# Four images of self-attention on one core: the last group's shared bank added before the next image's first projection

## Chip, core and metric

The kernel runs on one core of one Trainium2 chip. The metric is the device time of one execution in microseconds (us); the time before is the median of three executions. The engines are named as in the profile: PE is TensorE's matmul stream, PEld its weight loads, DVE is VectorE, ACT is ScalarE, POOL is GpSimd and SP is SyncE. GpSimd and SyncE mostly issue transfers here. [...]

## What is computed

Four images of 64 x 64 positions with 256 channels, in float32. Each is projected to queries and keys of 128 channels and values of 256, attends to itself with a softmax over 4096 positions, and is added to its input:

```python
q = jnp.einsum('bwhc,cd->bwhd', x, Wq) + bq
k = jnp.einsum('bwhc,cd->bwhd', x, Wk) + bk
v = jnp.einsum('bwhc,cd->bwhd', x, Wv) + bv
pq = q.reshape(B, -1, N)      # B = 4, N = 4096; a reshape, not a transpose
pk = k.reshape(B, -1, N)
pv = v.reshape(B, -1, N)
energy = jnp.einsum('bcn,bcm->bnm', pq, pk)
attention = jax.nn.softmax(energy, axis=-1)
out = jnp.einsum('bcm,bnm->bcn', pv, attention)
return gamma * out.reshape(B, W, H, C) + x
```

## The kernel before

The kernel splits each float32 operand into parts that TensorE can multiply as fp32r, so that a product becomes three matmuls. For each image it first projects 16 blocks `i` of the image (transposes on TensorE, then `qk`, then `v`), and then runs 16 groups `g` of 256 queries. A group takes 8 steps; a step computes energies and exponentials three steps ahead and attends with what is ready. The attention of a group collects in three PSUM banks: two sums `acc[0]`, `acc[1]` of the upper parts, and one bank `bb` that both halves of the queries share, for the difference part. At a group's last step ScalarE copies the two sums to `o`:

```python
# end of attend(b, u), at a group's last step
o = now["o"] = work.tile([P, NJ, C + 2], F32, tag="o", name=f"o_{b}_{g}")
for j in range(NJ):
    nc.scalar.activation(o[:, j, :], acc[j], AF.Identity, scale=1.0 + E)      # L385
```

The rest of a group's end is a generator, whose pieces are emitted one at a time between other work. `start` runs it to its first `yield`; each `proceed` emits the next piece:

```python
def start(pieces):
    active.append(pieces)
    next(pieces)

def proceed():
    for pieces in list(active):
        if next(pieces, StopIteration) is StopIteration:
            active.remove(pieces)

def finish(b, g, o, bb, xr):
    yield
    yield
    nc.vector.tensor_copy(zall[:, b * NG + g, :], o[:, :, C])                 # L398
    r, _ = factors(b, g, gam1)                       # L390 reciprocal, L391 multiply (DVE)
    nc.vector.tensor_tensor(o[:, :, :C], o[:, :, :C], bb, ALU.add)            # L400
    yield
    for j in range(NJ):
        nc.scalar.activation(                                                 # L403
            o[:, j, :C], o[:, j, :C], AF.Identity, scale=r[:, j : j + 1])
    yield
    yield
    tp = ps_t.tile([P, 2, NB], F32, tag="t", name=f"ot_{b}_{g}")
    for s in range(2):
        for j in range(NJ):
            nc.tensor.transpose(                                              # L411
                tp[:, s, j * P : (j + 1) * P], o[:, j, s * P : (s + 1) * P], ident)
    yield
    nc.vector.tensor_tensor(xr, xr, tp, ALU.add)                              # L415
    nc.gpsimd.dma_start(ov[b, g], xr)                                         # L416
```

The projection of one block, and the splitting of its keys, are these; `halved` makes the parts of a tile, the first on ScalarE and two on DVE:

```python
def transposed(self, i):                   # of Projection, cut
    for g in range(i, i + 2):
        self.load(g)                       # x of this block and the next, on SyncE (L82)
    ...                                    # four transposes on TensorE           (L124)
    nc.scalar.copy(self.xt[i], tp)         #                                       L130

def qk(self, i):                           # of Projection, cut
    ...                                    # matmuls                              (L137)
    nc.vector.tensor_tensor(dst, qk[...], bqk_sb[...], ALU.add)                 #  L146

def halved(f, x):
    h = f[:, :, 0, :]
    nc.scalar.activation(h, x, AF.Identity, scale=UPPER / 64)                   #  L263
    for j, s, op in ((1, -64.0, ALU.add), (2, 64.0 * (1.0 + E), ALU.subtract)):
        nc.vector.scalar_tensor_tensor(                                         #  L265
            f[:, :, j, :], h.bitcast(F32), s, x, ALU.mult, op)

def project_qk(b, i):
    images[b].qk(i)
    x = now["qk"]
    for s in range(2):
        nc.gpsimd.dma_start(qd[b, i // 2 + NG // 2 * s][:, i % 2, :], x[:, s, :C2])   # L273
    f = kpool.tile([P, 2, 3, P], F32R, tag="f", name=f"f_{b}_{i}", bufs=2)
    halved(f, x[:, :, C2:])
    nc.gpsimd.dma_start(kf[b, i // 2][:, i % 2], f.rearrange("p s j d -> p s (j d)")) # L276
```

The loop over the images puts these together. The first two blocks of an image are transposed, and the first is projected to q and k, at the end of the image before:

```python
for b in range(B):
    pr = images[b]
    ...                                    # b == 0: the same for the first image
    for i in range(1, NI):                 # the projections, NI = 16
        ...
        if i + 1 < NI:
            pr.transposed(i + 1)
        while i == 1 and active:
            proceed()                      # emits all that is left of the last group
        begin(b, i)
        project_qk(b, i)
        ...
        project_v(b, i - 1)                # matmuls L158, ScalarE L167
        proceed()
    project_v(b, NI - 1)
    for u in range(STEPS):                 # the attention, STEPS = 128
        ...
        attend(b, u)                       # matmuls L374
        if (b, u) == (B - 1, STEPS - 1):
            finish_last(b, g, loads.pop((b, "x", g)))
        elif t == NU - 1:
            start(finish(b, g, now["o"], now["bb"], loads.pop((b, "x", g))))
        proceed()
    if b + 1 < B:
        images[b + 1].transposed(1)
        project_qk(b + 1, 0)
```

For the PSUM tiles of these first blocks the kernel takes turns between the two double-buffered banks of the energies; from `i == 3` it uses the banks of the attention.

Of the kernel before, what the change touches and what calls it, by code (L numbers as in the profile page):

```python
# [20 lines left out]
def kernel(  # L21
# [58 lines left out]
    def load_x(pool, b, g):  # L80
        t = pool.tile([P, 2, XB], F32, tag="x", name=f"x_{b}_{g}")
        nc.sync.dma_start(t, xv[b, g])  # L82
        return t
# [117 lines left out]
    with ExitStack() as fast:  # L201
# [30 lines left out]
# [9 lines that stand above are left out]
        def image(b):  # L241
            def xt_out(i):
                return xtpool.tile([P, KC, 2, P], F32, tag="xt", name=f"xts_{b}_{i}")

            def qk_out(i):
                now["qk"] = work.tile([P, 2, 2 * C2], F32, tag="qk", name=f"qks_{b}_{i}")
                return ((now["qk"], 0),)

            def v_out(i):
                now["v4"] = work.tile([P, KC, C], F32, tag="v4", name=f"v4_{b}_{i}")  # L250
                return now["v4"], bv4_sb, 1.0 / E

            images.append(Projection(b, xpool, lambda: next(now["banks"]), xt_out, qk_out, v_out))

            for g in range(NG):
                qd[b, g] = dram.tile([P, NJ, P], F32, tag=f"qd{g}", name=f"qd_{b}_{g}")
            for t in range(NU):
                kf[b, t] = dram.tile([P, 2, 2, 3 * P], F32R, tag=f"kf{t}", name=f"kf_{b}_{t}")

        def halved(f, x):  # L260

            h = f[:, :, 0, :]
            nc.scalar.activation(h, x, AF.Identity, scale=UPPER / 64)  # L263
            for j, s, op in ((1, -64.0, ALU.add), (2, 64.0 * (1.0 + E), ALU.subtract)):
                nc.vector.scalar_tensor_tensor(  # L265
                    f[:, :, j, :], h.bitcast(F32), s, x, ALU.mult, op
# [11 lines that stand above are left out]
        def project_v(b, i):  # L278
            images[b].v(i)
            units[b, "v4", i] = now["v4"]  # L280
            if i < NI - 2:
                halve_v(b, i)
# [12 lines left out]
        def load_q(b, g):  # L295
            t = work.tile([P, NJ, P], F32, tag="qr", name=f"qr_{b}_{g}", bufs=1)
            nc.sync.dma_start(t, qd[b, g])
            loads[b, "qr", g] = t
# [12 lines left out]
        def energy(b, u, k):  # L311

            g, t = divmod(u, NU)
            if k == 0:
                x = ppool.tile([P, 4, NB], F32, tag="x", name=f"x_{b}_{u}", bufs=3)
                y = ppool.tile([P, 4, NB], F32, tag="y", name=f"y_{b}_{u}")
                units[b, u] = x, y
            x, y = units[b, u]
            q, kt = loads[b, "q", g], loads[b, "k", u]
            sa = ps_s.tile([P, 2, NJ, P], F32, tag="a", name=f"sa_{b}_{u}_{k}")  # L320
            sb = ps_s.tile([P, 2, NJ, P], F32, tag="b", name=f"sb_{b}_{u}_{k}")
            for i in range(2):
                for to, f, first, last in ((sa, 0, True, False), (sa, 1, False, True), (sb, 2, True, True)):
                    nc.tensor.matmul(  # L324
                        to[:, i], kt[:, 2 * k + i, f, :], q[:, f], start=first, stop=last
                    )
            for to, sp, scale in ((x, sa, (1.0 + E) / E), (y, sb, -1.0 / E)):
                nc.scalar.activation(  # L328
                    to[:, 2 * k : 2 * k + 2, :],
                    sp.rearrange("p i j d -> p i (j d)"),  # L330
                    AF.Exp,
                    scale=scale,
                )

        def join(b, u):

            x, y = units[b, u]
            nc.vector.tensor_tensor(x, x, y, ALU.mult)  # L338
            units[b, u] = x

        def upper(b, u):
            h = ppool.tile([P, 4, NB], F32R, tag="h", name=f"h_{b}_{u}", bufs=3)
            nc.scalar.activation(h, units[b, u], AF.Identity, scale=UPPER)  # L343
            units[b, u] = units[b, u], h

        def halves(b, u):
            x, h = units[b, u]
            l = ppool.tile([P, 4, NB], F32R, tag="l", name=f"l_{b}_{u}")
            nc.vector.tensor_tensor(l, x, h.bitcast(F32), ALU.subtract)  # L349

            d = ppool.tile([P, 4, NB], F32R, tag="d", name=f"d_{b}_{u}")
            nc.vector.scalar_tensor_tensor(  # L352
                d, h.bitcast(F32), 1.0 + E, x, ALU.mult, ALU.subtract
            )
            units[b, u] = h, l, d
# [106 lines left out]
        def begin(b, i):  # L462

            if i == 5:
                load_q(b, 0)
            if i == 9:
                halve_q(b, 0)
            if i in (4, 6, 8):
                load_k(b, i // 2 - 2)
            if i >= 10:  # L470
                energy(b, (i - 10) // 2, i % 2)
            if i in (12, 14):
                join(b, i // 2 - 6)
            if i in (13, 15):
                upper(b, i // 2 - 6)
                load_k(b, i // 2 - 3)

        image(0)
        for b in range(B):
            pr = images[b]  # L480
            if b == 0:
                now["banks"] = energies
                pr.transposed(0)
                pr.transposed(1)
                project_qk(b, 0)
            for i in range(1, NI):
                if i == 3:
                    now["banks"] = outputs
# [6 lines that stand above are left out]
                if i == NI - 1:  # L495
                    halves(b, 0)
                project_v(b, i - 1)
                proceed()
            project_v(b, NI - 1)
            for u in range(STEPS):  # L500
                g, t = divmod(u, NU)
                ahead = u + LOOK
                if ahead // NU + 1 < NG and ahead % NU == 3:
                    load_q(b, ahead // NU + 1)
                if u == STEPS - NU and b + 1 < B:
                    image(b + 1)
                if u >= STEPS - 3 and b + 1 < B:
                    now["banks"] = energies
                    if u == STEPS - 3:
                        images[b + 1].load(0)  # L510
                    elif u == STEPS - 2:
                        images[b + 1].transposed(0)
                if t == NU - 3:
                    loads[b, "x", g] = load_x(xpool, b, g)
                for k in range(2):
                    if ahead < STEPS:
                        energy(b, ahead, k)
                    if k == 0 and u + 2 < STEPS:
                        join(b, u + 2)
                        upper(b, u + 2)  # L520
                load_k(b, ahead + 2)
                proceed()
                if u + 1 < STEPS:
                    halves(b, u + 1)
                if ahead // NU + 1 < NG and ahead % NU == 5:
                    halve_q(b, ahead // NU + 1)

                if u in (1, 3):
                    halve_v(b, NI - 2 + u // 2)
                attend(b, u)  # L530
# [3 lines that stand above are left out]
                    start(finish(b, g, now["o"], now["bb"], loads.pop((b, "x", g))))  # L534
                proceed()
            if b + 1 < B:
                images[b + 1].transposed(1)
                project_qk(b + 1, 0)

    NB = 512  # L540
    NG = N // NB
# [132 lines left out]
```

## Time and profile before

| what | value |
|---|---|
| time, median of 3 | 2474.3 us (2473.92 to 2475.12) |
| profiled execution, first to last instruction | 2471.3 us |
| mean granted TensorE clock | 0.996 |
| TensorE matmul busy | 2447.6 us, 99% |
| VectorE busy | 2095.9 us, 85% |
| ScalarE busy | 1805.7 us, 73% |
| GpSimd busy | 425.7 us, 17% |
| bytes moved by DMA | 498.92 MB, mean 202 GB/s |

Busy time is what an engine's instructions cover; idle time of an engine that does not set the pace costs nothing. The wait list gives, for an instruction and what released it, the total, the number and the longest of the idle times. The granted clock is the share of TensorE's full clock that the chip allowed in a stretch. A line of the timeline gives the start, the duration, the engine, the line in the kernel, the operation, its output and inputs by name with their shapes, how many instructions are merged, and in brackets the idle time before it with its releaser. The line numbers L385 to L416 stand beside the code above.

### The profile page before, as it was taken

The numbers are of one execution on the slowest core, as the hardware profiler recorded it, in microseconds if no ns is written. First come the engines' busy times: TensorE is split into PE (matmuls) and PEld (weight loads), VectorE is DVE, ScalarE is ACT, GpSimd is POOL, SyncE is SP. The second block draws the span as 40 slices with busy tenths as digits, with TensorE's granted clock in tenths as the row PEclk, the third lists the DMA queues.
The fourth block names the chain that finished last, engine by engine and source line by source line (L and its number), as shares of the span: only waits on it lengthen the run. The fifth ranks groups of instructions, "written<-read, shape, count | busy, mean of one in ns | idle before, by whom it ended". The sixth has DMA issues, their size and how long they took to land.

```text
span 2471.3 us, 50024 instructions
## 1 busy us (share of the span) xinstructions
PE 2447.6 (99%) x19982; PEld 2412.5 (98%) x19982; DVE 2095.9 (85%) x2314; ACT 1805.7 (73%) x3201; POOL 425.7 (17%) x781
## 2 busy tenths in 40 slices
PE   9999999999999999999999999999999999999998
PEld 8999999999899999999989999999998999999998
DVE  5888888888698888888769888888876988888887
ACT  5777777776677777777657777777766777777775
POOL 4211111111411111111131111111114111111110
PEclk9999999999999999999999999999999999999999
DMA  7666666664766666666477666666647766666663
GB/s 234 220 204 204 208 206 205 198 211 144 237 215 198 206 210 204 207 202 207 142 226 216 204 201 209 204 211 201 207 141 224 224 205 198 208 206 205 209 201 111
DMA packets 137408, 498.92 MB, mean 202 GB/s; under 512 B 15536, under 2 KB 57264, under 8 KB 137168
## 3 DMA queue, kind: packets, MB, share of 16 engines
q0 software_dynamic: 92320, 453.17, 58.8%
q1 hardware_dynamic: 44304, 42.22, 5.6%
q8 instruction: 160, 2.62, 0.4%
q14 instruction: 80, 0.66, 0.1%
q10 hardware_dynamic: 544, 0.26, 0.0%
HBM read 445.25 MB, written 50.33 MB: 201 GB/s over the span
## 4 chain that ended last, share of the span: by engine, by line


## 5 line engine op out<-in xcount | busy, mean ns | idle before, releaser
L328 ACT ACTIVATE x<-sa 128x512 f32<-128x512 f32 x1024 | 612.9, 599 | 494.9 <-PE sa L324 491.7
L338 DVE TENSOR_TENSOR x<-x,y 128x1024 f32<-128x1024 f32 x512 | 626.4, 1223 | 188.0 <-ACT y L328 188.0
L324 PE MATMUL sa<-q,k 128*128 128x256 f32 x4096 | 736.6, 279 | 1.1 <-ACT x L328 1.1
L352 DVE SCALAR_TENSOR_TENSOR d<-h,x 128x1024 fp32r<-128x1024 f32 x512 | 624.4, 1219 | 0.0
L349 DVE TENSOR_TENSOR l<-x,h 128x1024 fp32r<-128x1024 f32 x512 | 624.3, 1219 | 0.0
L324 PEld LDWEIGHTS sa<-q,k 128*128 128x128 f32 x4096 | 619.5, 188 | 2.4 <-ACT x L328 1.9
L328 ACT ACTIVATE y<-sb 128x512 f32<-128x512 f32 x1024 | 614.6, 600 | 0.0
L374 PE MATMUL a<-vh,h 128*128 128x258 f32 x4096 | 574.4, 283 | 0.0
L374 PE MATMUL a<-vl,l 128*128 128x258 f32 x4096 | 572.8, 282 | 0.0
L324 PE MATMUL sb<-q,k 128*128 128x256 f32 x2048 | 567.6, 277 | 0.0
L343 ACT ACTIVATE h<-x 128x1024 fp32r<-128x1024 f32 x512 | 544.6, 1064 | 23.1 <-DVE x L338 19.2
L374 PE MATMUL bb<-vd,d 128*128 128x256 f32 x4096 | 558.6, 279 | 0.0
L308 POOL DMA_DIRECT2D k<-kf x512 | 280.0, 547 | 1575.4 <-PE sb L324 1550.4
L374 PEld LDWEIGHTS a<-vl,l 128*128 128x128 f32 x4096 | 525.3, 189 | 0.0
L374 PEld LDWEIGHTS a<-vh,h 128*128 128x128 f32 x4096 | 522.9, 189 | 0.0
L374 PEld LDWEIGHTS bb<-vd,d 128*128 128x128 f32 x4096 | 515.1, 188 | 0.0
L324 PEld LDWEIGHTS sb<-q,k 128*128 128x128 f32 x2048 | 384.5, 188 | 0.9 <-ACT y L328 0.8
L137 PE MATMUL qk<-wqk_sb,xts 128*128 128x256 f32 x512 | 124.4, 387 | 0.0
L158 PE MATMUL v<-xts,wv_sb 128*128 128x256 f32 x512 | 121.2, 381 | 0.0
L158 PEld LDWEIGHTS v<-xts,wv_sb 128*128 128x128 f32 x512 | 98.2, 192 | 13.7
L137 PEld LDWEIGHTS qk<-wqk_sb,xts 128*128 128x128 f32 x512 | 94.5, 194 | 10.7
L273 POOL DMA_DIRECT2D qd<-qks x128 | 69.1, 544 | 187.3 <-DVE qks L146 178.1
(56 smaller groups left out, 869.7 us busy)
## 6 DMA issues: line engine op xcount, KB each, us to landing
k<-kf POOLq DMA_DIRECT2D x512, 768.0 KB, 4.7
x<-in_x_dram SPq DMA_DIRECT2D x128, 256.0 KB, 3.4
kf<-f POOLq DMA_DIRECT2D x64, 384.0 KB, 3.7
out_dram<-x POOLq DMA_DIRECT2D x63, 256.0 KB, 2.5
qd<-qks POOLq DMA_DIRECT2D x128, 64.0 KB, 2.8
qr<-qd SPq DMA_DIRECT2D x64, 128.0 KB, 2.6
wv_sb<-in_L_conv_Wv_dram POOLq DMA_DIRECT2D x1, 256.0 KB, 5.8
out_dram<-x SPq DMA_DIRECT2D x1, 256.0 KB, 3.7
```

What stands on the lines that cost most here:

```text
L137: nc.tensor.matmul(qk[:, s, :], self.xt[i][:, k, s, :], wqk_sb[:, k, :], start=(k == 0), stop=(k == KC - 1),)
L158: nc.tensor.matmul(vp[:, eh, :], wv_sb[:, k, eh * P : (eh + 1) * P], self.xt[i][:, k].rearrange("p s a -> p (s a)"), start=(k == 0), stop= ...
L273: nc.gpsimd.dma_start(qd[b, i // 2 + NG // 2 * s][:, i % 2, :], x[:, s, :C2])
L308: nc.gpsimd.dma_start(t.rearrange("p (i s) f d -> p i s (f d)", s=2), kf[b, u % NU])
L324: nc.tensor.matmul(to[:, i], kt[:, 2 * k + i, f, :], q[:, f], start=first, stop=last)
L328: nc.scalar.activation(to[:, 2 * k : 2 * k + 2, :], sp.rearrange("p i j d -> p i (j d)"), AF.Exp, scale=scale,)
L338: nc.vector.tensor_tensor(x, x, y, ALU.mult)
L343: nc.scalar.activation(h, units[b, u], AF.Identity, scale=UPPER)
L349: nc.vector.tensor_tensor(l, x, h.bitcast(F32), ALU.subtract)
L352: nc.vector.scalar_tensor_tensor(d, h.bitcast(F32), 1.0 + E, x, ALU.mult, ALU.subtract)
L374: nc.tensor.matmul(out_, left[:, i, j * P : (j + 1) * P], right[:, m, : out_.shape[1]], start=(t == i == 0 and (left is h or left is d and ...
```

## The change

At the end of an image (but not of the last one) two `proceed()` are put around the next image's second block of transposes and first projection. The finishing group stands behind its first two `yield`s there. The first `proceed()` emits its third piece, the copy of the softmax sums, the factors and the add of the shared bank, ahead of the projection's work on DVE. The second emits the scaling on ScalarE behind the projection's. What is left, the transposes, the add to the input and the store, is emitted where it was, in the next image's first loop turn, behind the transposes of block 2. No instruction is added or left out. The purpose is that the shared bank, which is complete before the projection begins, is used at once.

```diff
@@ -534,8 +534,10 @@
                     start(finish(b, g, now["o"], now["bb"], loads.pop((b, "x", g))))
                 proceed()
             if b + 1 < B:
+                proceed()
                 images[b + 1].transposed(1)
                 project_qk(b + 1, 0)
+                proceed()
 
     NB = 512
     NG = N // NB
```

## The prediction

> **What bounds the kernel now.** I read the page's busy times first, then TensorE's waits, then the timeline at an image's end, then the granted clock there. The changed lines run only where `b + 1 < B`, so three times: at the ends of images 0, 1 and 2. The first line of the page says that TensorE is the bound and that almost nothing is left on it:
>
> ```profile
> PE 2447.6 (99%) x19982; PEld 2412.5 (98%) x19982; DVE 2095.9 (85%) x2314; ACT 1805.7 (73%) x3201; POOL 425.7 (17%) x781
> ```
>
> PE idles for 2471.3 - 2447.6 = 23.7 us in all. Its waits (us in total, times, longest) say on what; the largest one concerns exactly this change:
>
> ```profile
> PE ot L411 <- ACT o L403: 10.0, 3, 3.3
> PE wp L199 <- POOL ident masks.py:199: 2.4, 1, 2.4
> PE sa L324 <- ACT x L328: 1.1, 4, 0.3
> ```
>
> Three waits of 3.3 us: the transposes of the finished group (L411) wait for ScalarE's scaling (L403). They come 63 times; only the three at image ends wait. The timeline of the first image end shows why (start, duration, engine, line, then the idle time before it and its releaser):
>
> ```profile
> 615.19 1.09 PE L374 MATMUL bb<-vd,d 128*128 128x256 f32 x8
> ...
> 618.28 0.60 PE L124 MATMUL xt<-ident,x 128*128 128x128 f32 x4
> 618.48 0.69 DVE L146 TENSOR_TENSOR qks<-qk,bqk_sb 128x512 f32<-128x512 f32 x1 [6.00 <-PE qk L137]
> 619.21 0.42 ACT L263 ACTIVATE f<-qks 128x256 fp32r<-128x256 f32 x1 [1.87 <-DVE qks L146]
> ...
> 619.53 0.57 ACT L130 COPY xts<-xt 128x512 f32<-128x512 f32 x1
> 619.66 0.76 DVE L265 SCALAR_TENSOR_TENSOR f<-f,qks 128x256 fp32r<-128x256 f32 x2 [0.48 <-ACT f L263]
> 620.34 0.23 DVE L398 COPY zall<-o 128x2 f32<-128x2 f32 x1
> ...
> 620.88 0.68 DVE L400 TENSOR_TENSOR o<-o,bb 128x512 f32<-128x512 f32 x1
> ...
> 621.65 0.91 ACT L403 ACTIVATE o<-o,r 128x256 f32<-128x256 f32 x2 [1.55 <-DVE o L400]
> ...
> 622.21 0.95 PE L411 MATMUL ot<-ident,o 128*128 128x128 f32 x4 [3.33 <-ACT o L403]
> ```
>
> The bank `bb` is complete at 615.19 + 1.09 = 616.28, yet DVE adds it (L400) only at 620.88: it stands in DVE's program behind the next image's first projection (L146, L265), for which DVE sat idle 6.00 us. PE has nothing after its transposes at 618.88 until 622.21.
>
> The wait has a second price that the wait table does not show. The granted clock in 2 us stretches after the stall (us, busy times by engine, then PEclk, DMA share and GB/s) at the first, second and third image end:
>
> ```profile
> 622.00:624.00 2.00, 1.71 (x9) 1.42 (x10) 0.69 (x1) 0.56 (x2) 0.00 (x0) 1.00 0.57 197
> ...
> 1237.00:1239.00 2.00, 2.00 (x6) 1.56 (x5) 0.59 (x1) 0.00 (x0) 0.68 (x1) 0.50 0.00 0
> ...
> 1854.00:1856.00 2.00, 2.00 (x7) 1.55 (x6) 0.00 (x0) 0.00 (x0) 0.68 (x1) 0.50 0.27 96
> ```
>
> After the second and third stalls PE runs at half clock. From the first L411 transpose to the next image transpose (L124, x_3) took 622.21 to 626.46 = 4.25 us at the first end, 1235.56 to 1242.68 = 7.12 us at the second and 1852.14 to 1858.07 = 5.93 us at the third: 2.87 and 1.68 us more for the same instructions, 4.55 us in this execution.
>
> [...] two idle times of 3.33 us were followed by a clock of 0.50 and one was not. [...] L400 had all its inputs at 616.3 and started at 620.88, behind L265. [...] here the same 8 matmuls count 1.89 us at full clock and 3.62 us at half (second image end), both as "busy", so I look at the clock as well as at the gaps.
>
> **The change part by part.** Nothing is added or removed: the order of TensorE's, GpSimd's and the DMA queue's instructions is the same. On DVE, at three places, L398, L390, L391 and L400 move ahead of L146 and the two L265. On ScalarE the two L403 move ahead of the copy of x_2's transposes (L130), but remain behind the first projection's L263. Worked at the first end:
>
> - DVE: the two evacuations L385 start at 614.91 and take 0.87, to 615.78. L398 follows at about 615.8; from L398 to L400 was 0.54 us (620.34 to 620.88), so L400 is ready at 616.35 and bb is too (616.28). With a hand-over of 0.05 us: 616.4 to 617.1. PE delivers the first projection for L146 at 618.48 as before, so four instructions move into idle time, cost nothing, and leave DVE 1.4 us early.
> - ScalarE: L263 still starts at 619.21, because it waits for L146. L403 now takes the place that L130 had behind it, 619.53 instead of 621.65: 2.12 us earlier. The same subtraction gives 1234.99 - 1232.87 = 2.12 at the second end and 1851.58 - 1849.46 = 2.12 at the third.
> - PE: L411 began 622.21 - 621.65 = 0.56 us after L403, so now 619.53 + 0.56 = 620.09. The wait falls from 3.33 to 620.09 - 618.88 = 1.21 us. Three times 2.12 = 6.4 us.
> - The displaced L130 ends at about 619.53 + 0.91 + 0.57 = 621.0. Its reader, the third qk projection, began at 626.89 and would now begin at 624.77: 3.8 us of slack, no cost.
> - Clock: an idle time of 1.2 us lies far below those that led to 0.50. [...] the stretch from the last matmul of the first projection (about 618.44) to the first of the second (623.00 - 2.12 = 620.88) is 2.44 us, where it was 4.56. I expect full clock at all three ends: 4.55 us more.
>
> Sum: 6.4 + 4.55 = 10.9 us. The profiled execution took 2473.36 us and the median of the timed ones is 2474.3; I read the 0.9 us between them as mostly more half-clock time (they may have met half-clock at all three ends), which goes too. From 2473.36 this gives 2462.4, from the median 2463.4. I add 0.3 us for the transfer below and predict 2463.2.
>
> **The rivals.**
> 1. *Only the wait shrinks and the clock still falls.* The three 1.2 us gaps would cost what the longer ones did: 2474.3 - 6.4 = 2467.9. For it: I have only three gaps in this trace, one of which kept its clock. Against it: 1.2 us is a third of them.
> 2. *A transfer takes the wait's place.* The output store (L416) was issued at 624.18 and lands in 2.5 us, 626.7; a load queued behind it goes out at 626.73 and needs 3.3 us, 630.0, and TensorE transposes x_4 at 630.35, its weights from 630.13. That is 0.1 us of slack, and the store now comes 2.12 us earlier, close behind the store of the first keys (L276, 384 KB, issued at 620.94), which does not move. The chain from L411 to that load is unchanged and made the first end's x_4 just in time; but the second and third ends lose the slack that half clock gave them. Worth 0 to 1 us per end: up to 2466.
> 3. *Nothing is gained, as in other groups.* In 60 groups the same instructions run beside matmuls. But these three have a wait that PE itself shows, with no other wait under it: L411's only other input is the identity, and the instruction behind it (L137 on x_1, copied by 617.34) was ready.
> 4. *The bank's add blocks the first projection.* If bb came late, L146 and all behind it would slip. Against: PE computes bb before that projection, by 2.2 us. Even a slip of 1 us thrice is 3 us, still a gain.
>
> **Range and chances.** All half-clock time gone and no new wait gives 2461.5 to 2463.5; rival 2 moves it to 2466, rival 1 to 2468. Range 2460.8 to 2467.2. The whole idle time of PE is 23.7 us, 1% of the run, so a gain over 2% (below 2424.8) is out of reach; a loss of 50 us has no mechanism here.
>
> **What would show it.** In the changed kernel's profile: L400 at about 0.1 us after bb's last matmul, before L146; L403 immediately behind L263; three waits of L411 of about 1.2 us (3.6 in total instead of 10.0); a clock of 1.00 after all three; L146 waiting only for PE's projection. Waits of 3.3 us, or L403 still late, would refute the order argument; 0.50 after a 1.2 us gap would confirm rival 1; a wait of `xt` (L124) for the load of x would confirm rival 2.

## Result and profile after

The changed kernel takes 2463.9 us (median of 4, 2461.64 to 2464.62), the kernel before 2474.11 us (median of 4); the ratio is 0.9957, with a 95% interval of 0.9940 to 0.9974. A second measurement gave 2464.79 us and 0.9957 again. The prediction was 2463.2 us. The profiled execution spans 2461.6 us instead of 2471.3.

The first line of the page of the changed kernel:

```profile
PE 2444.7 (99%) x19982; PEld 2410.5 (98%) x19982; DVE 2096.1 (85%) x2314; ACT 1802.1 (73%) x3201; POOL 424.5 (17%) x781
```

The instruction counts are the same. PE's busy time fell by 2.9 us although it does the same work, and its idle time fell from 23.7 to 2461.6 - 2444.7 = 16.9 us: a busy PE at half clock had been part of the cost.

PE's waits in the changed kernel (us in total, times, longest; the three left out are as before):

```profile
PE ot L411 <- ACT o L403: 3.6, 3, 1.2
...
PE xt L124 <- DMA x<-in_x_dram: 0.3, 1, 0.3
```

The wait of the transposes L411 went from three times 3.3 us to three times 1.2. No wait took its place: the single wait of L124 for a load is at the kernel's start, as before.

The timeline of the changed kernel at the first image end (start, duration, engine, line, idle time and releaser):

```profile
616.96 1.09 PE L374 MATMUL bb<-vd,d 128*128 128x256 f32 x8
...
618.09 0.69 DVE L400 TENSOR_TENSOR o<-o,bb 128x512 f32<-128x512 f32 x1
...
618.32 1.89 PE L137 MATMUL qk<-wqk_sb,xts 128*128 128x256 f32 x8
...
620.05 0.60 PE L124 MATMUL xt<-ident,x 128*128 128x128 f32 x4
620.25 0.69 DVE L146 TENSOR_TENSOR qks<-qk,bqk_sb 128x512 f32<-128x512 f32 x1 [1.48 <-PE qk L137]
620.98 0.42 ACT L263 ACTIVATE f<-qks 128x256 fp32r<-128x256 f32 x1 [1.87 <-DVE qks L146]
...
621.30 0.89 ACT L403 ACTIVATE o<-o,r 128x256 f32<-128x256 f32 x2
...
621.85 0.95 PE L411 MATMUL ot<-ident,o 128*128 128x128 f32 x4 [1.19 <-ACT o L403]
622.10 0.56 ACT L130 COPY xts<-xt 128x512 f32<-128x512 f32 x1
```

The bank's add L400 starts 0.04 us after the bank is complete (616.96 + 1.09 = 618.05) and ends 1.5 us before DVE is wanted by L146. L403 stands directly behind L263, and L411 follows 0.55 us later.

The granted clock of the changed kernel in 2 us behind L411's wait, at the three ends (stretch, busy times, then PEclk, DMA share, GB/s):

```profile
622.00:624.00 2.00, 1.93 (x11) 1.60 (x11) 0.87 (x2) 0.66 (x2) 1.06 (x3) 1.00 0.71 232
...
1234.00:1236.00 2.00, 2.00 (x11) 1.74 (x10) 0.95 (x2) 0.00 (x0) 1.09 (x2) 1.00 0.90 314
...
1846.00:1848.00 2.00, 2.00 (x11) 1.77 (x10) 0.69 (x1) 0.24 (x1) 0.68 (x1) 1.00 0.87 302
```

It is 1.00 at all three, and the 8 matmuls of the projection behind the wait last 1.89 us each time. Before, they lasted 1.89, 3.62 and 3.50 us; the second of these:

```profile
1236.65 3.62 PE L137 MATMUL qk<-wqk_sb,xts 128*128 128x256 f32 x8
```

One measure serves from here on: at an image end, the time from the first matmul of the next image's first projection (L137) to the first transpose of its x_3 (L124). PE's instructions in this stretch are the same in both kernels. Before: 616.55 to 626.46, 1229.89 to 1242.68 and 1846.49 to 1858.07, which is 9.91, 12.79 and 11.58 us. After: 618.32 to 626.08, 1229.50 to 1237.26 and 1840.80 to 1848.56, three times 7.76. The sum falls from 34.28 to 23.28, by 11.0 us. The spans differ by only 9.7, and the rest is at the start of the kernel. These are PE's first projections there, before and then after:

```profile
7.58 1.89 PE L137 MATMUL qk<-wqk_sb,xts 128*128 128x256 f32 x8
9.31 0.60 PE L124 MATMUL xt<-ident,x 128*128 128x128 f32 x4
```

```profile
7.66 3.52 PE L137 MATMUL qk<-wqk_sb,xts 128*128 128x256 f32 x8
11.02 0.60 PE L124 MATMUL xt<-ident,x 128*128 128x128 f32 x4
```

In the changed kernel's profiled execution the first projection still ran at half speed; its x_2 is reached at 11.02 instead of 9.31 us, 1.7 us late, in code that the change does not touch. 11.0 - 1.7 = 9.3 of the 9.7 us.

### The profile page after: what moved, and what is told of

Its sections match the earlier page's. It is cut to its first block, busy times and chain, and to the rows that moved or that the text cites. A ratio compares the mean times of both kernels' runs of the same rounds, so it can differ in the third digit from the quotient of the medians.

```text
span 2461.6 us, 50024 instructions
## 1 busy us (share of the span) xinstructions
PE 2444.7 (99%) x19982; PEld 2410.5 (98%) x19982; DVE 2096.1 (85%) x2314; ACT 1802.1 (73%) x3201; POOL 424.5 (17%) x781
## 4 chain that ended last, share of the span: by engine, by line
## 5 line engine op out<-in xcount | busy, mean ns | idle before, releaser
L137 PE MATMUL qk<-wqk_sb,xts 128*128 128x256 f32 x512 | 122.6, 383 | 0.0
L137 PEld LDWEIGHTS qk<-wqk_sb,xts 128*128 128x128 f32 x512 | 93.4, 192 | 10.4
```

The costliest lines, as they stand in the source:

```text
L137: nc.tensor.matmul(qk[:, s, :], self.xt[i][:, k, s, :], wqk_sb[:, k, :], start=(k == 0), stop=(k == KC - 1),)
```

## Experiments

**The theory.** At three image ends TensorE paid twice for one order: a wait of 3.3 us on ScalarE's scaling, and half clock afterwards (0.50 in the clock column at two of the three). The early add shortens the wait to 1.2 us, which no longer brings half clock (1.00 at all three). **The rivals:** only the wait counts, and the full clock after the change was luck; the early add on DVE is worth something in itself; the half clock costs nothing by itself; and, for what is left of the wait, another wait lies right under it. Each run was compared with the kernel before on its own chip (medians 2475.1 to 2475.8 there).

### The changed kernel again

> The changed kernel once more, for a comparison on one chip. Theory (the wait of L411 shrinks by 2.1 us at three image ends, and the half clock behind it goes): 2463.5 us, ratio 0.9957, waits of L411 3.6 us in all, clock 1.00 behind each. Rival (only the wait counts and the clock of the first comparison was luck): 2468 in most executions, ratio 0.9974.

Measured: 2464.79 us, 0.9957 (0.9943 to 0.9970). Waits of L411 3.6 us in all; the three stretches are 7.76 us again (617.55 to 625.31 at the first). The 8 matmuls behind the wait take 1.89 us at all six ends of the two profiles.

### Only the first of the two calls

```diff
 if b + 1 < B:
     proceed()
     images[b + 1].transposed(1)
     project_qk(b + 1, 0)
-    proceed()
```

> Only the first of the two added calls: the bank's add goes ahead of the projection on DVE, the scaling L403 stays behind the copy L130 of x_2 on ScalarE. Theory: L403 starts one L130 later than in the changed kernel, about 0.5 us (0.57 us of L130, overlapped a little), so L411 waits 1.7 us instead of 1.2 at each end, the clock stays at 1.00, and the time is 1.5 us above the changed kernel's: 2465.4. Rival (both calls are needed, the scaling's place on ScalarE is what matters): waits near 3.3 us and 2474.

Measured: 2466.48 us (2465.46 to 2470.69), 0.9963 (0.9949 to 0.9976). The first call carries most of the gain. The wait came as expected, 1.7 us at each end. The clock did not. PE in this kernel at the first, the second (the projection alone) and the third image end:

```profile
624.16 1.21 PE L411 MATMUL ot<-ident,o 128*128 128x128 f32 x4 [1.68 <-ACT o L403]
625.17 3.35 PE L137 MATMUL qk<-wqk_sb,xts 128*128 128x256 f32 x8
```

```profile
1238.21 2.75 PE L137 MATMUL qk<-wqk_sb,xts 128*128 128x256 f32 x8
```

```profile
1851.16 0.95 PE L411 MATMUL ot<-ident,o 128*128 128x128 f32 x4 [1.68 <-ACT o L403]
1851.94 1.89 PE L137 MATMUL qk<-wqk_sb,xts 128*128 128x256 f32 x8
```

The same wait was followed by half clock at the first two ends (3.35 and 2.75 us for the 8 matmuls; 0.50 and 0.52 in the clock column from 625 to 627 and from 1239 to 1241 us) and not at the third (1.89 us; 1.00 from 1853 to 1855). The stretches are 9.93, 9.93 and 8.25 us: half clock cost 1.68 us at each of two ends. So half clock can follow a wait of 1.7 us, here at two of three ends. The profiled execution is the slowest of the five (2470.69 us), so two ends in three may be more than is usual.

### The wait made longer again, with the add still early

```diff
 # finish(), between the add and L403; 2, 4 or 8 times
+if g == NG - 1:
+    w = ppool.tile([P, 4, NB], F32, tag="y", name=f"w_{b}")
+    for _ in range(2):
+        nc.scalar.activation(w[:, :NJ, :], o[:, :, :C], AF.Identity, scale=0.5)
```

> The changed kernel with 2 extra ScalarE instructions (128x512, written to a tile that nobody reads) ahead of L403 at the three image ends: the bank's add stays early, but the scaling is late by about 2 x 0.53 = 1.07 us, and L411 waits 2.3 us. Theory: three times 1.07 us, and the clock stays at 1.00 because 2.3 us is well under the 3.3 us that sometimes brought half clock: 2463.5 + 3.2 = 2466.7. Rival (the clock falls in proportion to any gap): up to 2.9 us more at an end, 2470 or more.

> The same with 4 extra instructions: L411 waits about 1.2 + 2.1 = 3.3 us again, as in the kernel before, though the bank's add on DVE is early. Theory (the wait on TensorE carries the whole gain): back to the kernel before, 2463.5 + 6.4 + 4.5 = 2474.4, with half clock at some ends. Rival (the early add on DVE is worth something by itself): under 2470.

> The same with 8 extra instructions: L411 waits about 1.2 + 4.3 = 5.5 us. Theory: half clock behind all three ends, 2.9 us each at most: 2463.5 + 12.8 + 8.7 = 2485. Rival (half clock comes by chance, not by the gap's length): full clock at one end or more, 2476 to 2482.

Measured: 2471.64 us with 2 extra instructions (0.9985, 0.9977 to 0.9993), 2477.72 with 4 (1.0007, 1.0000 to 1.0014), 2483.97 with 8 (1.0036, 1.0023 to 1.0049). PE's waits for the scaling in the three kernels (its lines are four further down here):

```profile
PE ot L415 <- ACT o L407: 7.6, 3, 2.5
```

```profile
PE ot L415 <- ACT o L407: 11.5, 3, 3.8
```

```profile
PE ot L415 <- ACT o L407: 19.5, 3, 6.5
```

The extra instructions delayed the scaling by 0.66 to 0.67 us each and not 0.53, so the waits are 2.5, 3.8 and 6.5 us instead of 2.3, 3.3 and 5.5. With 4 of them the whole gain is gone while L400 stands in DVE's program where the changed kernel has it: the early add is worth nothing by itself, PE's wait carries it all. With 2 the clock fell, against my expectation, at two of three ends (0.55 in the clock column from 1237 to 1239 us, 0.50 from 1852 to 1854), as the 1.7 us of the run above had already suggested, and the time is the rival's, above 2470. Here is the projection behind the wait in that kernel at its third end:

```profile
1851.58 3.58 PE L137 MATMUL qk<-wqk_sb,xts 128*128 128x256 f32 x8
```

The stretch gives the half-clock cost of each end, if one takes off 7.76 - 1.19 = 6.57 us for the work and the kernel's own wait:

| kernel (wait of L411) | stretches, us | half-clock cost, us |
|---|---|---|
| changed, two profiles (1.2) | 7.76 six times | 0 |
| first call only (1.7) | 9.93, 9.93, 8.25 | 1.7, 1.7, 0 |
| 2 extra (2.5) | 9.09, 10.77, 10.77 | 0, 1.7, 1.7 |
| before (3.3) | 9.91, 12.79, 11.58 | 0, 2.9, 1.7 |
| 4 extra (3.8) | 11.91, 13.12, 11.92 | 1.5, 2.7, 1.5 |
| 8 extra (6.5) | 15.49, 14.97, 14.58 | 2.4, 1.9, 1.5 |

The cost does not grow with the wait, as that rival had it: it is 0 or between 1.5 and 2.9 us. What grows is how often it comes: never in 6 ends at 1.2 us, two times in three from 1.7 to 3.3, always at 3.8 and 6.5 us. At those two waits the clock is read from the durations alone (3.07 to 3.62 us for the 8 matmuls). With three ends for most kernels this is a tendency, not a rate: the profile with the first call only is a slow execution of its kernel, and that of the kernel before (2473.36 us, where the medians are 2474.1 to 2475.8) a fast one.

### The wait filled, the order before

These kernels separate the two prices. They keep the kernel before and its chain to L403, and give PE something to do while it waits; the extra matmuls compute nothing that is used.

```diff
 # finish() of the kernel before, ahead of L411; 13 times, then 7 times
 tp = ps_t.tile([P, 2, NB], F32, tag="t", name=f"ot_{b}_{g}")
+if g == NG - 1:
+    for _ in range(13):
+        nc.tensor.matmul(tp[:, 0, :], ident, wqk_sb[:, 0, :], start=True, stop=True)
```

> The kernel before with its order unchanged, but with 13 matmuls of 128x256 that compute nothing of use put on TensorE ahead of L411 at the three image ends, written into L411's own bank, which L411 then overwrites. They fill about 2.8 us of the 3.3 us wait and leave the chain to L403 as it is. Theory (half clock is a second price of its own): no time is saved in the wait, but the clock stays at 1.00 at all three ends, and the time falls by 4 to 6 us to about 2469.5. Rival (the half clock has another cause, or costs nothing): same as before, 2474.

Measured with 13: 2475.37 us, 1.0001 (0.9992 to 1.0009). Taken by its number this says for the rival. The trace says that the filling was too long. PE at the first end:

```profile
619.59 5.78 PE L411 MATMUL ot<-wqk_sb,ident 128*128 128x256 f32 x26
625.21 0.60 PE L414 MATMUL ot<-ident,o 128*128 128x128 f32 x4
```

Each of these float32 matmuls stands twice in the trace, as the projection's 4 stand as 8, which I had overlooked. They lasted to 625.21, about 2 us beyond the old wait, three times. That cost hid what the full clock saved: the stretches are 11.68, 11.67 and 11.67 us, with 1.89 us for the 8 matmuls of the projection each time, and their sum is 0.7 us above that of the kernel before. The clock did stay full, but the time alone decides nothing. The filling was cut to 7:

> The kernel before with a filling that fits. In the filled kernel before it, each of the 13 matmuls stands twice in the trace[...], so they took 26 x 0.216 = 5.6 us and outlasted the 3.3 us wait; 7 take 14 x 0.216 = 3.0 us and end before L403 delivers. Theory (half clock is a second price of its own): L411 starts when it did before, 0.3 us or so is still waited, the clock stays full at all three ends, and the time is that of the kernel before less its half-clock time, 4 to 5 us: about 2470.5 to 2471. Rival (the half clock behind the wait costs nothing by itself): 2475.5, same as before.

Measured: 2470.71 us, 0.9979 (0.9970 to 0.9988). The same place, with 7:

```profile
621.43 3.19 PE L411 MATMUL ot<-wqk_sb,ident 128*128 128x256 f32 x14
624.92 0.95 PE L414 MATMUL ot<-ident,o 128*128 128x128 f32 x4 [0.30 <-ACT o L403]
625.71 1.89 PE L137 MATMUL qk<-wqk_sb,xts 128*128 128x256 f32 x8
```

The stretches are 9.90, 9.90 and 9.89 us: the first end of the kernel before (9.91), at all three. Nothing of the wait was saved, and 2475.12 - 2470.71 = 4.4 us came from the clock alone (3.0 to 7.4 us by the interval), where the prediction had 4.55. The clock column shows 1.00 in all 11 stretches of 2 us read at the three ends. The half clock is a second price, and its predicted size lies in that interval.

### The wait filled in the changed kernel and in the one with the first call only

The same edit, with 2 and with 3 matmuls:

> The changed kernel with 2 such matmuls (4 x 0.216 = 0.86 us) in its remaining wait of 1.2 us. Theory (a wait of 1.2 us brings no half clock, in the timed executions too): same as the changed kernel, 2464.8 and its scatter. Rival (some timed executions of the changed kernel meet half clock behind 1.2 us, as one end of the kernel with only the first call did behind 1.7 us): 1 to 2 us less, 2463.5, and less scatter.

Measured: 2464.82 us (2462.61 to 2465.85), 0.9951 (0.9938 to 0.9965): same as the changed kernel's 2464.79. The stretches are 7.76, 7.77 and 7.77 us. There is no sign that timed executions of the changed kernel meet half clock at the ends; a rare fall would not show in a scatter of 3 us. (The kernel with the first call only had met it at two ends, not at one.)

> The kernel with only the first call, with 3 such matmuls (6 x 0.216 = 1.3 us) in its wait of 1.7 us. Theory: half clock behind 1.7 us, which its profile showed at two of three ends, goes; what stays is the later start of L403: 2464.8 + 1.5 = 2466.3, and no execution near 2470. Rival (those two ends had another cause): executions of 2468 to 2470 still occur.

Measured: 2464.26 us (2464.18 to 2464.35), 0.9953 (0.9940 to 0.9967). No execution is near 2470, and all five are below the fastest of the unfilled kernel (2465.46), which ran on another chip. The half clock at the ends is only a part of the difference: of the 6.5 us between the two profiled executions (2468.8 and 2462.3), 3.4 lie in the three stretches (8.25 us at each end now) and 2.8 ahead of the first one, which begins at 617.35 instead of 620.15: the kernel's first projection had taken 3.62 us and takes 1.89 in this profile. The start can also explain why the median is 2 us under the expected 2466.3 although L403 is as late as expected: the profile of the changed kernel with 2 matmuls, on the same chip, has a half-clock start (3.62 us for its first projection) and reaches its first stretch at 620.36. The small scatter of the five would fit a full-clock start in each; whether they had it, and why, is open.

### The scaling ahead of the projection

```diff
 if b + 1 < B:
     proceed()
     images[b + 1].transposed(1)
+    proceed()
     project_qk(b + 1, 0)
-    proceed()
```

> The second call moved up, between the transposes of x_1 and the first projection, so that the scaling L403 stands ahead of L263 on ScalarE as well. Theory: L403 runs at about 0.3 to 1.2 us after x_1's copy, before the projection's L146 ends; L411 finds its input ready, the remaining 1.2 us wait and the 0.3 us between its first and second transpose go, 4.5 us over three ends: 2459.3. Rival (another wait stands right under it, x_2's load or the copy L130): no gain over the changed kernel, 2463.5, with a wait of L124 or L137 in its place.

Measured: 2459.47 us (2458.01 to 2459.92), 0.9933 (0.9919 to 0.9946). L403 uses ScalarE's idle time before L263, directly behind x_1's copy. The first end in this kernel's timeline:

```profile
620.04 0.91 ACT L403 ACTIVATE o<-o,r 128x256 f32<-128x256 f32 x2
...
621.09 0.60 PE L124 MATMUL xt<-ident,x 128*128 128x128 f32 x4
...
621.53 0.60 PE L411 MATMUL ot<-ident,o 128*128 128x128 f32 x4
...
622.02 0.42 ACT L263 ACTIVATE f<-qks 128x256 fp32r<-128x256 f32 x1 [1.06 <-DVE qks L146]
```

L411 runs into L124's end without a wait; the stretch is 6.06 us (619.36 to 625.42) instead of 7.76, 5.1 us over three ends where 4.5 were expected. The expected 2459.3 holds, and nothing lay under the wait.

### The start

The 1.7 us that the changed kernel's profile lost lie at the start, and the scatter of the timed executions may lie there too. Two runs give the kernel above matmuls at PE's start, from 1.05 us on, in place of transposes that begin at 2.43 us:

```diff
-for _ in range(12):
-    nc.tensor.transpose(wp, ident, ident)
+for _ in range(18):                  # then 12
+    nc.tensor.matmul(wp, ones, ones, start=True, stop=True)
```

> The kernel with the scaling ahead of the projection, and with 18 matmuls of the tile of ones in place of the 12 of the identity at the kernel's start, which can begin at about 1.0 us (L88) instead of 2.4 us. Theory: TensorE reaches full clock before the first projection, whose 8 matmuls (L137) then always take 1.9 us and not sometimes 3.5 us as in the changed kernel's profile; the median falls by about 1 us under the kernel with the scaling ahead (to about 2458.3) and the scatter between executions shrinks from 3 us to 1.5. Rival (the start waits for its loads, not for the clock): no difference.

> The kernel with the scaling ahead of the projection, and at its start 12 matmuls of the tile of ones, which can begin at 1.05 us, instead of 12 transposes of the identity, which begin at 2.4 us; the run with 18 of them showed them twice each and lasting until 7.0 us, past the first load. 12 end at about 1.05 + 24 x 0.17 = 5.1 us, when the first transposes began before. Theory: first projection at full clock (1.9 us) in every execution and nothing late: 2459.5 - 1.2 = about 2458, never above 2459. Rival (the loads set the start anyway, the second load landed at 6.8 to 8.4 us in the profiles): no difference from 2459.5.

Measured: 2458.58 us with 18 (0.9932, 0.9919 to 0.9946) and 2457.79 with 12 (2457.56 to 2458.34; 0.9928, 0.9914 to 0.9941). The start of the latter:

```profile
1.05 5.49 PE L199 MATMUL wp<-ones 128*128 128x128 f32 x24 [1.05 <-DVE ones L88]
6.64 0.63 PE L124 MATMUL xt<-ident,x 128*128 128x128 f32 x4
7.94 0.66 PE L124 MATMUL xt<-ident,x 128*128 128x128 f32 x4 [0.67 <-DMA x<-in_x_dram]
8.43 1.89 PE L137 MATMUL qk<-wqk_sb,xts 128*128 128x256 f32 x8
```

The 12 matmuls lasted until 6.54 us and not 5.1, so the first transposes began later, at 6.64 instead of 5.31 us; PE still had to wait for the second load, until 7.94. The first projection takes 1.89 us (1.99 with 18), where it took 3.00 us with the scaling ahead alone. The executions lie within 0.8 us with 12 and 1.6 with 18, where they lay within 1.9; but those of the first call with 3 matmuls in the wait lay within 0.2 us with the old start, so that these matmuls narrow the scatter is not shown. The median is 1.7 us lower than with the scaling ahead alone, but the two stand on different chips and their intervals overlap: the gain is only likely. This is the lowest median of the study.

## Why the prediction was right

**The sum held term by term.** L400, predicted 0.1 us behind the bank, stands 0.04 behind it. L403 directly behind L263, predicted; found. The wait of L411, predicted at 1.21 us: 1.19. The three ends, predicted to give 6.4 + 4.55 = 10.9 us: 11.0. The clock term was checked by itself in the kernel with 7 matmuls in the wait: 4.4 us. That 2463.9 lies within 0.7 us of the predicted 2463.2 is partly luck: the clock term was read from one execution, the number of falls varies, and a start at half clock adds 1.7 us or more that the sum does not have.

**One reason was weaker than it was written.** The prediction called 1.2 us "far below" the idle times that led to half clock. Half clock followed waits of 1.7 us too, at two of three ends. The stretch in which only transposes run, which the prediction also looked at, says the same. From the start of x_2's transposes to the next projection it lasts 620.05 to 622.63 = 2.58 us in the changed kernel; with the first call only it lasts 3.06 us at the second and the third end, of which one lost its clock and one kept it, and 3.29 us at the first, whose last part was already at half clock (the four transposes of L411 took 1.21 us instead of 0.95). No run separates the transposes from the wait, so what they add to it is not shown. The shortest wait with half clock behind it, 1.7 us, is 0.5 us above the changed kernel's 1.2; the prediction had compared 1.2 with 3.3.

**The transfer did not show.** For rival 2, a load that takes the wait's place, 0.3 us were added. In the changed kernel no L124 waits for a load behind the start, though all three ends now run at full clock, the pace that left 0.1 us of slack at the first end before.

**The 0.9 us between the profiled execution and the median** were read as more half-clock time at the ends. That is not shown, and the start is as good a candidate: it alone makes 1.7 us. It moved the centre by less than the scatter.

## What to carry to other kernels

When a matmul stream waits on a chain of small instructions, look in each engine's program for what stands ahead of the chain although it is ready later; moving the ready work up cost nothing here, where DVE had sat idle for 6.00 us. Price such a wait twice: its length, and the clock of the matmuls behind it, which the wait list does not show: here three waits of 3.3 us, and 2.9 and 1.7 us of half clock behind two of them. After the move, look at the next engine of the chain: here the second engine's order was worth another 5 us of the same kind.

## What was not expected of the hardware

With the first call only, a wait of 1.7 us was followed by half clock at two of three ends, and the cost of one such fall was 1.5 to 2.9 us with no growth from the 1.7 us wait to the 6.5 us one.

The clock column does not show half clock at the start: in the changed kernel the stretch from 8 to 10 us has a granted clock of 1.00, while the projection in it takes 3.52 us where 1.89 is full speed. At the start the durations are the evidence.

```profile
8.00:10.00 2.00, 2.00 (x6) 1.56 (x5) 0.00 (x0) 0.48 (x1) 0.45 (x2) 1.00 0.71 204
```
